# Attention, expert and relative-attention layers on one core: the first ten groups of heads in written order on all engines, with the expert weights' loads among them and zero products on TensorE ahead

## The chip, the cores and the metric

The kernel runs on one core of one Trainium2 chip. A core has TensorE (PE, matrix products, with a sequencer of weight loads shown as PEld), VectorE (DVE), ScalarE (ACT), GpSimd (POOL) and SyncE (SP, which here issues transfers). The metric is the time of one execution on the device in microseconds (us); a kernel's time is the median of its runs. A second figure, the span, runs from the first to the last instruction of the profiled execution.

## The reference

An input x of 16 batches x 256 tokens x 128 channels goes through four layers, each added back to x and each fed by a layer norm of x. All arithmetic is in float32.

```python
x = x + attn_a(layernorm(x))   # 16 heads of 8 channels, weights alpha * sign(W)
x = x + ffn(layernorm(x))      # 8 experts of 512, gates cut at the k-th value of all logits
x = x + attn_b(layernorm(x))   # 16 heads, relative position embedding
x = x + ffn(layernorm(x))
# attn_a:
Wb = mean(abs(W), axis=1) * (W + (sign(W) - W))
q, k, v = (split_heads(x @ Wb.T + b) for ...)
y = softmax(q @ k.T * 8**-0.5) @ v;  out = y @ Wpb.T + bp
# ffn:
gates = logits * (logits >= kth_value_of_all_logits)
out = sum over e of gates[e] * (gelu(x @ w1[e].T + b1[e]) @ w2[e].T + b2[e])
```

The expert weights w1 and w2 are the same in both ffn layers, 2 MB each.

## The kernel before

The program is one straight stream of instructions per engine, with semaphores between them. It loads x as 16 tiles (x0 to x15, one a batch), and keeps all of x and all weights in SBUF. Constants and small vectors come as one tile, `head`.

Attention a (the function `attention_a`) works in 64 *groups*: group i is batch i // 4 and four of its 16 heads (j = 0 to 3), each in 32 rows of PE's array. For group i the code issues

- `scores`: eight products q by k (tile a_s), and on DVE one maximum per head (a_nm, L356);
- one group later, in `visit`, `maxima`: PE turns the maxima (a_mx) and DVE adds them to q (a_qa, L371);
- two groups later `exponentials`: eight products with the sides exchanged (a_t, L379) and the exponential on ACT (a_pT, L385);
- every second group, `values`: 32 products with a_va, a tile of values spread into the 32-row places of the heads.

Beside that, `visit` puts in each batch's own steps by the table at L492: `project` (q and k of the next batch; ACT writes a_qkc, SP sends it to DRAM and, in four transfers, back into the spread tile a_qk), `project_v` and `channels`, `tokens`, `turn_back`, `project_out`, and the gate's steps. `normalise(b)` makes the layer norm of a batch: statistics and aggregates on DVE (L138, L139), then `ve` and `rstd` on POOL (L142, L143), then `xn` on POOL, or for batch 0 on DVE (L146).

Ahead of group 0 stands a preparation. POOL clears wS_q, wS_k, the maxima's tiles a_nm and three tiles a_va, and fills two spread tiles a_qk (L198, L199). DVE makes the signs of the weights in `weights` (sgn_qk, and for values and output sgn_vp): the sign in two instructions, two of `sign - W + W`, one multiply by alpha per weight. PE turns the result (wT_qk, L253), DVE writes it spread into wS_q and wS_k (L257), ACT writes it plain as wq and wk (L263). Batch 0 is turned (a_lnT, L279), copied as a_xnT, and projected by `project_first` (a_pq and a_pk, L315) directly into its spread tile, four products for q and four for k, with biases bqs_ and a_bk_. At group 2 the value and output weights' turned signs (wT_vp) are made and batch 0's values projected (a_pv, L334).

What sets the order: PE's instructions stand in the order in which the code issues them (`manual_schedule` for PE covers all of attention a). POOL's order is written for its first fills and normalisations only. All other engines' orders are chosen by the framework's scheduler, which moves an instruction forward when it takes its operands to be there. Each engine then executes strictly in its own order. The loads of x go over SP's queue one after the other, then b_w (the second attention's weights, 256 KB), w1 and w2; a_w0, head, a_bp and b_bo go over ACT's queue.

After attention a come the first expert layer (h_unit L983 and y_unit L994, 128x512 products, with a search for the k-th logit on DVE at its start), attention b and the second expert layer. In the search the tile flips is a cast of the constants `digits` (L1047), once in each expert layer.

Of the kernel before, what the change touches and what calls it, by code (L numbers as in the profile page):

```python
# [77 lines left out]
def hybrid_kernel(ctx: ExitStack, tc: tile.TileContext, io):  # L78
# [20 lines left out]
            a_w.append(load("a_w1", [P, 2, C], nc.sync, io["a_w"][:, 2:4]))  # L99
    a_bp = load("a_bp", [P, C], nc.scalar, io["a_bp"].partition_broadcast(P))  # L100
    b_bo = load("b_bo", [P, C], nc.scalar, io["b_bo"].partition_broadcast(P))
    b_w = load("b_w", [P, 4, C], nc.sync)
    w1 = load("w1", [P, NE * HID], nc.sync)
    w2 = load("w2", [P, NE * NHC, C], nc.sync)
    wb = {n: b_w[:, i, :] for i, n in enumerate("qkvo")}

    def const(name):
# [18 lines left out]
    def evac(dst, src, on_act):  # L126
        if on_act:
            nc.scalar.copy(dst, src)
        else:
            nc.vector.tensor_copy(dst, src)  # L130

    def normalise(b, last=None):

        n = T // P
        stats = small.tile([P, n, 6], F32, tag="stats", name=f"stats{b}")
        mv = small.tile([P, n, 2], F32, tag="mv", name=f"mv{b}")
        for t in range(n):
            nc.vector.bn_stats(stats[:, t, :], xs[b][:, t, :])  # L138
            nc.vector.bn_aggr(mv[:, t, :], stats[:, t, :])  # L139
        ve = small.tile([P, n], F32, tag="ve", name=f"ve{b}")  # L140
        rstd = small.tile([P, n], F32, tag="rstd", name=f"rstd{b}")
        nc.gpsimd.tensor_scalar(ve, mv[:, :, 1], EPS, None, ALU.add)  # L142
        nc.gpsimd.tensor_tensor(rstd, ve, power, ALU.pow)  # L143
        xn = small.tile([P, n, C], F32, tag="xn", name=f"xn{b}")
        for t in range(n):
            (last or nc.gpsimd).tensor_scalar(  # L146
                xn[:, t, :], xs[b][:, t, :], mv[:, t, 0:1], rstd[:, t : t + 1],
                ALU.subtract, ALU.mult,
            )
        return xn  # L150
# [28 lines left out]
    def attention_a(place, filling):  # L179
# [4 lines left out]
        with ExitStack() as st:  # L184
# [34 lines left out]
                    "p m (j e) -> p m j e", e=32  # L219
                )  # L220

            wS, nms = {}, []
            with tc.manual_schedule(engines={mybir.EngineType.Pool}):
# [9 lines left out]
                with tc.high_priority():  # L233
                    xns = {0: normalise(0, nc.vector)}
                xns[1] = normalise(1)

            def weights(names, w, spread_too):

                alpha = small.tile([P, 2], F32, tag="alpha", name=f"alpha_{names}")
                nc.vector.tensor_reduce(  # L240
                    alpha, w, AX.X, ALU.add, apply_absolute_value=True
                )
                nc.vector.tensor_scalar(alpha, alpha, 1.0 / C, None, ALU.mult)
                s = pool.tile([P, 2, C], F32, tag="sg", name=f"sgn_{names}")
                nc.vector.tensor_scalar(s, w, 0.0, 1.0, ALU.is_gt, ALU.subtract)
                nc.vector.scalar_tensor_tensor(s, w, 0.0, s, ALU.is_ge, ALU.add)

                nc.vector.tensor_tensor(s, s, w, ALU.subtract)
                nc.vector.tensor_tensor(s, s, w, ALU.add)
                pt = psum.tile([P, 2, T], F32, tag="x", name=f"wT_{names}", bufs=8)[:, :, 0:C]  # L250
                for i, n in enumerate(names):
                    nc.vector.tensor_scalar(s[:, i], s[:, i], alpha[:, i : i + 1], None, ALU.mult)
                    nc.tensor.transpose(pt[:, i, :], s[:, i, :], ident)  # L253
                for i, n in enumerate(names):
                    scale = SCALE if n == "q" else 1.0
                    if spread_too:
                        nc.vector.tensor_scalar(  # L257
                            wS[n][:, :, :, 1 : 1 + DH],
                            pt[:, i].rearrange("p (g j d) -> p g j d", g=NG, j=NJ),
                            scale, None, ALU.mult,  # L260
                        )
                    wT[n] = wpool.tile([P, C], F32, tag=f"w{n}", name=f"w{n}")
                    nc.scalar.activation(wT[n], pt[:, i], AF.Copy, scale=scale)  # L263

            bq = wpool.tile([P, 1], F32, tag="bqs", name="bqs")
            nc.vector.tensor_scalar(bq, a_bq, SCALE, None, ALU.mult)
            bq_ = wpool.tile([P, NG], F32, tag="bqs_", name="bqs_")
            nc.vector.tensor_scalar(bq_, a_bq_, SCALE, None, ALU.mult)

            q, k, va, xnT, qaug, probs, heads, ys, yTs = ({} for _ in range(9))  # L270

# [5 lines left out]
            def channels(b, pt):  # L277
                for t in range(2):
                    nc.tensor.transpose(pt[:, t * P : (t + 1) * P], xns[b][:, t, :], ident)  # L279
                yield  # L280
                xnT[b] = pool.tile([P, T], F32, tag="xnT", name=f"a_xnT{b}")
                evac(xnT[b], pt, b > 0)

            def project(b):

# [20 lines left out]
            def project_first():  # L306

                to = spread[0]
                q[0], k[0] = to[:, 0], to[:, 1]
                for half in range(2):  # L310
                    for i, (n, bias) in enumerate((("q", bq_), ("k", a_bk_))):
                        pp = psum.tile([P, 2, T], F32, tag="x", name=f"a_p{n}_{half}", bufs=8)
                        for j in range(2):
                            g = 2 * half + j
                            nc.tensor.matmul(  # L315
                                pp[:, j, :], wS[n][:, g].rearrange("p j e -> p (j e)"),
                                xnT[0], start=True, stop=True,
                            )
                        for j in range(2):
                            g = 2 * half + j  # L320
                            if i:
                                nc.vector.tensor_scalar(
                                    to[:, i, g], pp[:, j, :], bias[:, g : g + 1], None, ALU.add
                                )
                            else:
                                nc.scalar.activation(
                                    to[:, i, g], pp[:, j, :], AF.Identity,
                                    bias=bias[:, g : g + 1], scale=1.0,
                                )

            def project_v(b, pv):
                pv = pv.rearrange("p (t c) -> p t c", c=C)
# [149 lines left out]
            spread_tile(False)  # L482
            together(channels(0, half_bank("a_lnT0")))
            weights("qk", a_w[0], True)
            project_first()
            for i in range(2):
                spread_tile(True)
                values_tile()
# [35 lines left out]
            for i in range(NG * (NB + 2) + 1):  # L524
                b, s = divmod(i, NG)
                for half in range(2):
                    parts = []
                    if i < n:
                        parts += [scores(i, 2 * half + j) for j in range(2)]
                    if 2 <= i < n + 2:  # L530
                        parts += [exponentials(i - 2, 2 - 2 * half + j) for j in range(2)]
                    together(*parts)
                    if not i and not half:
                        together(channels(1, half_bank("a_lnT1")))
                if i >= n + 2:
                    place["h"] = (epool, 5, psum, "x", 8)
                    place["y"] = (psum, "x", 8)
                    place["raw"] = (epool, 4)
                    for _ in range(own_at.get(i - n, 0)):
                        own.append(next(filling))  # L540
                if i == 2:
                    weights("vp", a_w[1], False)
                    pv = psum.tile([P, 2, T], F32, tag="x", name="a_pv0", bufs=8)
                    together(project_v(0, pv[:, 0]))
                visit(i)
                if i == 0:
                    xns[2] = normalise(2)
                if s == 3 and of(b + 3):
                    xns[b + 3] = normalise(b + 3)

# [469 lines left out]
    def experts(last, place, raw, filling, middle):  # L1020
        with ExitStack() as st:
# [19 lines left out]
            def search():  # L1041
# [1 line left out]


                digits = const("digits")
                flips = small.tile([P, len(SHIFTS) * NCAND], I32, tag="flips", name="flips", bufs=1)
                nc.vector.tensor_copy(flips, digits)  # L1047

                pc = count((0.0, 2.0, -2.0 + 2.0**-23), "s")
                ok = small.tile([P, 3], F32, tag="ok_s", name="ok_s")  # L1050
# [234 lines left out]
```

## Time and profile before

| | |
|---|---|
| three timed runs | 1556.63, 1557.60, 1558.27 us; median 1557.6 |
| profiled execution | 1556.52 us |
| its span | 1554.7 us |
| PE busy | 1522.4 us (98%) |
| DVE busy | 814.6 us (52%) |
| ACT busy | 833.0 us (54%) |
| POOL busy | 404.3 us (26%) |
| granted clock of PE, mean | 0.999 |
| read from and written to DRAM | 50.88 MB, 12.58 MB |

A line of the page or of an answer names the engine, the line of the kernel, the operation, and output<-inputs by the program's names without buffer numbers. In a timeline a line starts with the start and the duration of a merged run of instructions, in us, and ends with the idle time before it and what ended it. In a table of stages each engine has its busy time and in brackets its number of instructions; PEclk is the clock that PE was granted, 1.00 being full; then follow the mean busy share of the 16 DMA engines and what they moved in GB/s. A matmul in float32 stands in the trace as two records, so "x4" are two products.

### The profile page before, as it was taken

What the parts mean: (1) busy time and instruction counts of PE and PEld (TensorE: products, weight loads), DVE (VectorE), ACT (ScalarE), POOL (GpSimd) and SP (SyncE); (2) the same over time, 40 slices, a digit from 0 to 9 for tenths busy, and PEclk for the clock granted to TensorE, in tenths of its full rate; (3) what the DMA queues carried; (4) which work ended last, traced back from release to release, by engine and by line L of the source; (5) the groups of instructions that cost most, each with busy time, mean ns of one, the idle gap of its engine ahead of it and who ended that gap; (6) DMA issues with size and microseconds to landing.
All of it is one profiled execution on the core that took longest, in us unless ns stands there. A gap on an engine that the chain in (4) does not pass through costs nothing. (4 is left out here: it accounts for less than half of the span.)

```text
span 1554.7 us, 30891 instructions
## 1 busy us (share of the span) xinstructions
PE 1522.4 (98%) x12274; PEld 857.3 (55%) x12274; DVE 814.6 (52%) x1646; ACT 833.0 (54%) x2073; POOL 404.3 (26%) x518
## 2 busy tenths in 40 slices
PE   5999999999999999999999999999999999999998
PEld 3777777644444444444577777777544444444444
DVE  5788878635224322221599999999364133222122
ACT  2666666544443343434588888888644434343342
POOL 6123322100001000003188888897100000000000
PEclk9999999999999999999999999999999999999999
DMA  6111111000322211111122222222002233221110
GB/s 197 29 36 35 29 29 36 9 8 0 71 58 72 68 37 38 40 35 41 22 53 47 47 53 56 54 52 44 8 1 39 54 78 88 56 44 40 46 40 7
DMA packets 174127, 69.91 MB, mean 45 GB/s; under 512 B 74520, under 2 KB 173600, under 8 KB 173728
## 3 DMA queue, kind: packets, MB, share of 16 engines
q1 hardware_dynamic: 173408, 67.54, 18.7%
q8 instruction: 97, 1.59, 0.4%
q10 hardware_dynamic: 576, 0.41, 0.1%
q14 instruction: 46, 0.38, 0.1%
HBM read 50.88 MB, written 12.58 MB: 41 GB/s over the span
## 5 line engine op out<-in xcount | busy, mean ns | idle before, releaser
L985 ACT ACTIVATE hT<-ph,head 128x512 f32<-128x512 f32 x512 | 351.3, 687 | 420.8 <-PE ph L983 418.3
L983 PE MATMUL ph<-xn,w 128*128 128x512 f32 x1024 | 464.5, 594 | 1.1 <-ACT hT L985 1.1
L994 PE MATMUL py<-hT,w 128*128 128x512 f32 (+1 forms) x1040 | 461.3, 586 | 1.0 <-ACT logits L884 0.5
L994 PEld LDWEIGHTS py<-hT,w 128*128 128x128 f32 x1040 | 196.6, 190 | 237.3 <-issue 230.5
L983 PEld LDWEIGHTS ph<-xn,w 128*128 128x128 f32 x1024 | 191.3, 190 | 228.0 <-issue 224.2
L1110 DVE SCALAR_TENSOR_TENSOR gy<-py,head,gb 128x512 f32<-128x512 f32 x82 | 61.6, 751 | 425.4 <-PE py L994 419.2
L798 ACT ACTIVATE b_pr<-b_s,b_nm 128x256 f32<-128x256 f32 x512 | 235.9, 474 | 58.8 <-DVE b_nm L793 58.6
L356 DVE TENSOR_REDUCE a_nm<-a_s 128x2 f32<-128x512 f32 x256 | 160.4, 686 | 55.3 <-PE a_t L379 37.3
L793 DVE TENSOR_REDUCE b_nm<-b_s 128x4 f32<-128x1024 f32 x128 | 152.7, 1193 | 16.5 <-PE b_s L783 16.4
L783 PE MATMUL b_s<-b_kT,b_qd 64*64 64x256 f32 x1024 | 159.9, 382 | 0.4 <-ACT b_pr L798 0.2
L385 ACT ACTIVATE a_pT<-a_t 128x512 f32<-128x512 f32 x256 | 133.2, 599 | 48.2 <-PE a_t L379 47.5
L808 DVE STREAM_TRANSPOSE b_pT<-b_pr 128x1024 f32<-128x1024 f32 x128 | 157.2, 1228 | 0.0
L783 PE MATMUL b_s<-strip,b_qb 64*64 64x256 f32 x2048 | 156.6, 376 | 0.0
L783 PE MATMUL b_s<-b_kS,b_qd 64*64 64x256 f32 x1024 | 156.5, 382 | 0.0
L351 PE MATMUL a_s<-a_qk 32*128 32x256 f32 x1024 | 135.1, 391 | 0.0
L673 POOL TENSOR_TENSOR b_qd<-b_qsel,head 128x512 f32<-128x512 f32 x64 | 84.2, 1337 | 179.4 <-DMA b_qsel<-b_qT 170.7
L142 POOL TENSOR_SCALAR ve<-mv 128x2 f32<-128x2 f32 x64 | 15.0, 234 | 442.6 <-DVE mv L139 441.9
L379 PE MATMUL a_t<-a_qa,a_qk 32*128 32x256 f32 x1024 | 122.9, 397 | 3.5 <-DVE a_qa L371 2.7
L798 ACT ACTIVATION_READ_ACCUMULATOR b_pr<-b_s,b_nm 128x1 f32 x512 | 104.3, 204 | 0.0
L351 PEld LDWEIGHTS a_s<-a_qk 32*128 32x128 f32 x1024 | 91.7, 186 | 22.5 <-issue 15.2
L146 POOL TENSOR_SCALAR xn<-x,mv,rstd 128x128 f32<-128x128 f32 x126 | 99.8, 801 | 6.1
L783 PEld LDWEIGHTS b_s<-strip,b_qb 64*64 64x64 f32 x2048 | 78.3, 133 | 32.2
(175 smaller groups left out, 1438.9 us busy)
## 6 DMA issues: line engine op xcount, KB each, us to landing
gb<-gd SPq DMA_DIRECT2D x128, 256.0 KB
w<-in_w SPq DMA_DIRECT2D x2, 2048.0 KB
a_qks<-a_qkc SPq DMA_DIRECT2D x15, 256.0 KB
a_qk<-a_qks SPq DMA_DIRECT2D x60, 64.0 KB
x<-in_x SPq DMA_DIRECT2D x16, 128.0 KB
b_qs<-b_qT SPq DMA_DIRECT2D x64, 32.0 KB
b_qsel<-b_qT SPq DMA_DIRECT2D x64, 32.0 KB
b_z<-b_qs SPq DMA_DIRECT2D x16, 128.0 KB
```

What stands on the lines that cost most here:

```text
L146: (last or nc.gpsimd).tensor_scalar(xn[:, t, :], xs[b][:, t, :], mv[:, t, 0:1], rstd[:, t : t + 1], ALU.subtract, ALU.mult,)
L351: nc.tensor.matmul(sc[:, t, :], q[b][rows, g, t * P : (t + 1) * P], k[b][rows, g, :], start=True, stop=True,)
L356: nc.vector.tensor_reduce(nms[G % 4][:, :, j, 0:1].rearrange("p t o -> p (t o)"), sc, AX.X, ALU.max, negate=True,)
L379: nc.tensor.matmul(sc[:, t, :], k[b][rows, g, t * P : (t + 1) * P], qaug[G][rows, :], start=True, stop=True,)
L385: nc.scalar.activation(pT, sc, AF.Exp)
L783: nc.tensor.matmul(sc[64 * c : 64 * c + 64, r, u, :], (qb_[rows, at, c] if rel else qd[rows, at, x]).rearrange("p h q -> p (h q)"), strip[ ...
L793: nc.vector.tensor_reduce(nm, sc, AX.X, ALU.max, negate=True)
L798: nc.scalar.activation(pr[:, u, r, :], sc[:, r, u, :], AF.Exp, bias=nm[:, r, u : u + 1], scale=1.0, accum_out=sums[b][:, n : n + 1],)
L808: nc.vector.transpose(pT[:, half % 2, 4 * i : 4 * i + 4].rearrange("p n k h q -> p (n k h q)"), probs.pop(U).rearrange("p u r k -> p (u r ...
L983: nc.tensor.matmul(ph, w1[:, m * P : (m + 1) * P], xn2[c], start=True, stop=True)
L985: nc.scalar.activation(hT, ph, AF.Gelu_apprx_tanh, bias=b1[:, m : m + 1], scale=1.0)
L994: nc.tensor.matmul(py[:, 0:width], w2[:, e * NHC + k, :], hs[k], start=k == 0, stop=k == NHC - 1)
```

## The change

The preparation becomes one function, `begin`, and from there until group 10 DVE, ACT, POOL and SP too execute in the order in which the code issues their instructions; `written.close()` ends that at group 10. The written order is: the fills on POOL up to the first a_va; five products on PE of the cleared tile wS_q by itself into a tile that nobody reads; statistics of batch 0 and the start of the signs of q and k on DVE; batch 0's `xn`, on DVE, in another form of instruction; its turning on PE and copy, now on ACT; the rest of the signs, with one multiply by alpha for both weights instead of one each; biases; batch 1's normalisation; wS_q and wS_k; the projections, with the two parts of the value and output weights' signs between them. Their multiply by alpha and their turning come at group 2. Spread tiles 1 and 2 and a_va 1 and 2 are filled after batch 1's normalisation.

Batch 2 is normalised after group 1 instead of after group 0. b_w and w1 are loaded at group 5, w2 at group 9, where flips is now also cast, once for both expert layers. In every normalisation the statistics of both halves now come ahead of both aggregates.

```diff
-    b_w = load("b_w", [P, 4, C], nc.sync)
-    w1 = load("w1", [P, NE * HID], nc.sync)
-    w2 = load("w2", [P, NE * NHC, C], nc.sync)
+    b_w = cpool.tile([P, 4, C], F32, tag="b_w", name="b_w")
+    w1 = cpool.tile([P, NE * HID], F32, tag="w1", name="w1")
+    w2 = cpool.tile([P, NE * NHC, C], F32, tag="w2", name="w2")
+    flips = cpool.tile([P, len(SHIFTS) * NCAND], I32, tag="flips", name="flips")
+    def load_later(step):
+        for name, t in ((("b_w", b_w), ("w1", w1)), (("w2", w2),))[step]:
+            nc.sync.dma_start(t, io[name])
+        if step:
+            nc.vector.tensor_copy(flips, const("digits"))
...
+    def statistics(b):
...
         for t in range(n):
             nc.vector.bn_stats(stats[:, t, :], xs[b][:, t, :])
+        for t in range(n):
             nc.vector.bn_aggr(mv[:, t, :], stats[:, t, :])
...
-            def weights(names, w, spread_too):
+            def weights(names, w):
...
                 nc.vector.scalar_tensor_tensor(s, w, 0.0, s, ALU.is_ge, ALU.add)
+                yield
                 nc.vector.tensor_tensor(s, s, w, ALU.subtract)
                 nc.vector.tensor_tensor(s, s, w, ALU.add)
+                yield
+                nc.vector.tensor_tensor(
+                    s, s, alpha.unsqueeze(2).to_broadcast([P, 2, C]), ALU.mult
+                )
                 pt = psum.tile([P, 2, T], F32, tag="x", name=f"wT_{names}", bufs=8)[:, :, 0:C]
+                for i in range(2):
+                    nc.tensor.transpose(pt[:, i, :], s[:, i, :], ident)
+                yield pt
...
+            def begin():
+                fills()
+                warm = psum.tile([P, 2, T], F32, tag="x", name="a_warm", bufs=8)
+                for _ in range(5):
+                    nc.tensor.matmul(
+                        warm[:, 0], wS["q"][:, 0].rearrange("p j e -> p (j e)"),
+                        wS["q"][:, 0:2].rearrange("p g j e -> p (g j e)"),
+                        start=True, stop=True,
+                    )
+                mv, rstd = statistics(0)
+                qk = weights("qk", a_w[0])
+                next(qk)
+                xns[0] = small.tile([P, T // P, C], F32, tag="xn", name="xn0")
+                for t in range(T // P):
+                    nc.vector.scalar_tensor_tensor(
+                        xns[0][:, t, :], xs[0][:, t, :], mv[:, t, 0:1],
+                        rstd[:, t : t + 1].to_broadcast([P, C]), ALU.subtract, ALU.mult,
+                    )
+                together(channels(0, half_bank("a_lnT0")))
+                next(qk)
+                pt = next(qk)
+                nc.vector.tensor_scalar(bq, a_bq, SCALE, None, ALU.mult)
+                nc.vector.tensor_scalar(bq_, a_bq_, SCALE, None, ALU.mult)
+                xns[1] = normalise(1)
...
+                keep("qk", pt)
+                vp = weights("vp", a_w[1])
+                spread_tile(False)
...
+                        if i:
+                            next(vp)
...
+                return vp
...
-                evac(xnT[b], pt, b > 0)
+                nc.scalar.copy(xnT[b], pt)
...
-            weights("qk", a_w[0], True)
-            project_first()
+            written = st.enter_context(ExitStack())
+            written.enter_context(
+                tc.manual_schedule(
+                    engines={
+                        getattr(mybir.EngineType, e) for e in ("DVE", "Activation", "Pool", "SP")
+                    }
+                )
+            )
+            vp = begin()
...
-                    weights("vp", a_w[1], False)
+                    keep("vp", next(vp))
...
-                if i == 0:
+                if i == 1:
                     xns[2] = normalise(2)
+                if i in (5, 9):
+                    load_later(i // 9)
+                if i == 10:
+                    written.close()
...
-                flips = small.tile([P, len(SHIFTS) * NCAND], I32, tag="flips", name="flips", bufs=1)
-                nc.vector.tensor_copy(flips, digits)
```

Left out of `begin` are the two instructions on DVE that write wS_q and wS_k, and the loop of the former `project_first`, in which the two `next(vp)` stand between the products for k and the copies out of them.

More of the change, by code (lines that the diff above doesn't have):

```diff
@@ L130, in evac @@
             nc.vector.tensor_copy(dst, src)
-    def normalise(b, last=None):
+    def statistics(b):
         n = T // P
@@ L143, in normalise @@
         nc.gpsimd.tensor_tensor(rstd, ve, power, ALU.pow)
-        xn = small.tile([P, n, C], F32, tag="xn", name=f"xn{b}")
-        for t in range(n):
+        return mv, rstd
+    def normalise(b, last=None):
+        mv, rstd = statistics(b)
+        xn = small.tile([P, T // P, C], F32, tag="xn", name=f"xn{b}")
+        for t in range(T // P):
             (last or nc.gpsimd).tensor_scalar(
@@ L220, in of_heads, with fills @@
                 )
-            wS, nms = {}, []
-            with tc.manual_schedule(engines={mybir.EngineType.Pool}):
+            wS, nms, xns = {}, [], {}
+            bq = wpool.tile([P, 1], F32, tag="bqs", name="bqs")
+            bq_ = wpool.tile([P, NG], F32, tag="bqs_", name="bqs_")
+            def fills():
                 for n in "qk":
@@ L232, in attention_a @@
                 values_tile()
-                with tc.high_priority():
-                    xns = {0: normalise(0, nc.vector)}
-                xns[1] = normalise(1)
-            def weights(names, w, spread_too):
+            def weights(names, w):
                 alpha = small.tile([P, 2], F32, tag="alpha", name=f"alpha_{names}")
@@ L251, in weights, with keep @@
+                yield pt
+            def keep(names, pt):
                 for i, n in enumerate(names):
[L252 to L261, printed above, removed]
-                    wT[n] = wpool.tile([P, C], F32, tag=f"w{n}", name=f"w{n}")
-                    nc.scalar.activation(wT[n], pt[:, i], AF.Copy, scale=scale)
@@ L265, in attention_a @@
[L265 to L268, printed above, removed]
+                    wT[n] = wpool.tile([P, C], F32, tag=f"w{n}", name=f"w{n}")
+                    nc.scalar.activation(
+                        wT[n], pt[:, i], AF.Copy, scale=SCALE if n == "q" else 1.0
+                    )
@@ new lines, in begin @@
+            def begin():
[11 more added lines that the diff above has]
+                xns[0] = small.tile([P, T // P, C], F32, tag="xn", name="xn0")
+                for t in range(T // P):
+                    nc.vector.scalar_tensor_tensor(
[8 more added lines that the diff above has]
+                xns[1] = normalise(1)
+                for i, n in enumerate("qk"):
+                    nc.vector.tensor_scalar(
+                        wS[n][:, :, :, 1 : 1 + DH],
+                        pt[:, i].rearrange("p (g j d) -> p g j d", g=NG, j=NJ),
+                        SCALE if n == "q" else 1.0, None, ALU.mult,
+                    )
+                keep("qk", pt)
+                vp = weights("vp", a_w[1])
+                spread_tile(False)
+                to = spread[0]
+                q[0], k[0] = to[:, 0], to[:, 1]
+                for half in range(2):
+                    for i, (n, bias) in enumerate((("q", bq_), ("k", a_bk_))):
+                        pp = psum.tile([P, 2, T], F32, tag="x", name=f"a_p{n}_{half}", bufs=8)
+                        for j in range(2):
+                            g = 2 * half + j
+                            nc.tensor.matmul(
+                                pp[:, j, :], wS[n][:, g].rearrange("p j e -> p (j e)"),
+                                xnT[0], start=True, stop=True,
+                            )
+                        if i:
+                            next(vp)
+                        for j in range(2):
+                            g = 2 * half + j
+                            if i:
+                                nc.vector.tensor_scalar(
+                                    to[:, i, g], pp[:, j, :], bias[:, g : g + 1], None, ALU.add
+                                )
+                            else:
+                                nc.scalar.activation(
+                                    to[:, i, g], pp[:, j, :], AF.Identity,
+                                    bias=bias[:, g : g + 1], scale=1.0,
+                                )
+                return vp
@@ L304, in project @@
                 q[b], k[b] = to[:, 0], to[:, 1]
[L306 to L329, printed above, removed]
             def project_v(b, pv):
@@ L481, in attention_a @@
             n, own = NB * NG, []
-            spread_tile(False)
-            together(channels(0, half_bank("a_lnT0")))
-            weights("qk", a_w[0], True)
-            project_first()
+            written = st.enter_context(ExitStack())
[4 more added lines that the diff above has]
+                    }
+                )
+            )
+            vp = begin()
             for i in range(2):
```

## The prediction

> **What bounds the kernel now.** I read the page's busy shares first, then the stages, then the first 36 us engine by engine.
>
> ```profile
> PE 1522.4 (98%) x12274; PEld 857.3 (55%) x12274; DVE 814.6 (52%) x1646; ACT 833.0 (54%) x2073; POOL 404.3 (26%) x518
> ```
>
> TensorE (PE) is busy for all but 32.3 us of 1554.7. So a change can win idle time, or time in which PE is slow; the stages tell where either is (columns: us; busy PE, weight loads, DVE, ACT, POOL with counts; clock, DMA share, GB/s).
>
> ```profile
> 0.00:15.54 15.54, 0.00 (x0) 0.00 (x0) 9.19 (x39) 1.28 (x1) 13.54 (x30) 1.00 0.81 209
> 15.54:22.00 6.46, 5.98 (x22) 4.52 (x22) 2.34 (x8) 2.11 (x6) 6.17 (x10) 1.00 1.01 426
> 22.00:30.00 8.00, 6.04 (x49) 3.85 (x52) 6.27 (x11) 1.23 (x4) 4.21 (x6) 0.98 0.45 180
> 30.00:36.00 6.00, 4.97 (x41) 4.05 (x37) 2.85 (x5) 2.90 (x7) 0.00 (x0) 0.74 0.25 34
> 40.00:50.00 10.00, 9.87 (x138) 6.73 (x132) 5.88 (x11) 5.75 (x12) 0.00 (x0) 1.00 0.18 46
> ```
>
> From group 3, at 36.2 us, PE is full and stays so. All that can be won in one place lies before. PE's waits there:
>
> ```profile
> PE a_lnT L279 <- DVE xn L146: 15.5, 1, 15.5
> PE a_t L379 <- DVE a_qa L371: 2.0, 1, 2.0
> PE a_pv L334 <- ACT wv L263: 1.0, 1, 1.0
> PE a_pq L315 <- DVE wS_q L257: 0.5, 1, 0.5
> ```
>
> PE's first work waits until DVE has normalised batch 0. DVE's timeline tells why that is late:
>
> ```profile
> 3.65 0.49 DVE L138 BATCH_NORM_STATS2 stats<-x 128x6 f32<-128x128 f32 x2 [3.65 <-DMA x<-in_x]
> 8.87 0.29 DVE L138 BATCH_NORM_STATS2 stats<-x 128x6 f32<-128x128 f32 x1 [2.64 <-DMA x<-in_x]
> 11.13 2.07 DVE L252 TENSOR_SCALAR sgn_qk<-sgn_qk,alpha_qk 128x128 f32<-128x128 f32 x2
> 14.47 0.47 DVE L252 TENSOR_SCALAR sgn_vp<-sgn_vp,alpha_vp 128x128 f32<-128x128 f32 x2
> 15.14 0.60 DVE L146 TENSOR_SCALAR xn<-x,mv,rstd 128x128 f32<-128x128 f32 x2
> ```
>
> The statistics come at 3.65, and POOL ends rstd at 6.61 (5.89 + 0.72). Between lie a wait for a later batch (2.64), scaling of signs beside POOL's copy and memset (2.07, where its twin takes 0.47), and value weights and statistics that nobody needs yet. So about 8.5 us is order alone. PE's timeline, last:
>
> ```profile
> 17.18 2.04 PE L315 MATMUL a_pq<-a_xnT,wS_q 128*128 128x256 f32 x4 [0.48 <-DVE wS_q L257]
> 20.11 1.03 PE L315 MATMUL a_pq<-a_xnT,wS_q 128*128 128x256 f32 x4
> 21.93 1.13 PE L351 MATMUL a_s<-a_qk 32*128 32x256 f32 x8
> 26.95 0.70 PE L351 MATMUL a_s<-a_qk 32*128 32x256 f32 x4
> 29.61 0.73 PE L379 MATMUL a_t<-a_qa,a_qk 32*128 32x256 f32 x2 [1.96 <-DVE a_qa L371]
> 36.21 0.48 PE L351 MATMUL a_s<-a_qk 32*128 32x256 f32 x2
> ```
>
> The same projection takes 2.04 at first and 1.03 three microseconds later, so PE starts at half rate, though the clock column reads 1.00 there. After the 1.96 us wait it falls to half again:
>
> ```profile
> 29.00:30.00 1.00, 0.39 (x4) 0.42 (x8) 0.47 (x2) 0.00 (x0) 0.00 (x0) 0.86 0.24 72
> 30.00:31.00 1.00, 1.00 (x14) 0.98 (x13) 0.17 (x1) 0.00 (x0) 0.00 (x0) 0.50 0.57 90
> 33.00:34.00 1.00, 0.66 (x4) 0.20 (x2) 0.70 (x2) 0.62 (x2) 0.00 (x0) 0.93 0.09 16
> ```
>
> 0.28 + 3 + 0.14 = 3.42 us at 0.50.
>
> **The change part by part**, as times at which PE reaches four marks: first projection (17.18 before), first scores (21.93), first exponentials' product a_t (29.61), group 3 (36.21).
>
> *First projection.* Statistics start at 3.65 as before; both aggregates end at 4.4. POOL: ve 0.23, rstd 0.72 and three hand-overs of 0.1 end at 5.6. Beside it DVE does the sign start of q and k: reduce 0.39, scale 0.15, 0.30, 0.41, to 5.65. The normalisation in its new form isn't in the trace: taken at its old 0.60 per pair (bounds 0.5 and 0.8, twice the 256-wide form at 0.41), to 6.25. PE turns it in 0.44 (row at full rate) to 0.73 (at half rate); ACT, idle for 13.15 us there, copies it in 0.37: ready by 7.4, hidden. DVE goes on: 0.41, 0.48 and one 256-wide multiply (0.41 as its neighbours) to 7.55; PE turns the weights (0.44 to 0.63) to 8.1. DVE meanwhile has two small biases (0.12 each; the second was 0.83 beside POOL's copy, which now comes later) and batch 1's statistics (0.46 + 0.3), to 8.55; wS_q 0.29, hand-over 0.15: 9.0. Gain 8.2, or 7.5 with the bias at 0.83.
>
> *The zeros.* Five 128x256 products. The row at 17.18 makes one 0.92 at half rate (1.83 for two, up to the next start at 19.01), so 4.6 us after wS_q is cleared (0.75 + 0.53 = 1.28): 1.4 to 6.0, before the first transpose at 6.3. No delay. Do they raise the clock for the projections? Between 6.0 and 9.0 PE has two short bursts, 0.9 to 1.4 us of work in 3. Before, 1.5 us of work in the 3.4 ahead of 29.72 was followed by half rate. So I expect the clock to be won and mostly lost again: projections take 4.75 as before (17.18 to 21.93, 2.3 of it at half rate). Bounds: 8 x 0.43 = 3.5 at full rate (the row at 20.11), 8 x 0.92 = 7.3 at half rate. Scores at 13.75.
>
> [...]
>
> *Scores to a_t.* DVE's order is kept: four reductions, four more, then a_qa. So 7.68 stays, and with it the wait of 1.96. The two-input sign steps now run beside POOL's fills: up to 1.1 more (the 2.07 row less 0.47, per instruction 0.8, rounded up), of which DVE's 0.83 of idle ahead of the second four takes most. Nothing taken, 0.8 kept in the range. a_t at 21.45.
>
> *a_t to group 3.* Before 6.60, at half rate, with the value weights' signs long done. Now their last multiply stands on DVE behind group 2's reductions, and PE's transposes, wv and project_v wait for it, with the maxima of group 1 queued behind on PE. At half rate the reductions end 5.0 after a_t (33.30 + 1.29 less 29.61), the multiply at 5.4, transposes at 5.9, wv at 6.3, and 1.52 from project_v to group 3 (34.69 to 36.21): 7.9. At full rate the reductions end at 3.7: 6.5. The same gap as before speaks for half rate, its position in a 3.4 us window is open: 7.4 taken. Group 3 at 28.83 instead of 36.21: **7.4 gained**.
>
> *What I cost at nothing.* Batch 2's statistics on DVE move in front of group 2's reductions, batches 3 and 4 behind groups 3 and 7: 0.56 + 0.34 = 0.9 each, in DVE's idle of 1.23 and 1.56 before the reductions of groups 3 and 4; without that cover up to 2.7. POOL's fills (7.5 us from 11.2) end at 18.7; batch 1's spread needs the first at 20.5, and batch 2's normalisation (2.8) ends near 25, needed at 28. ACT's order changes by one copy. On SP b_w and w1 go behind batch 2's five transfers, w2 behind batch 3's; the first matmul on w1 is at 306.4, so they have 240 us. SP waits for none of them. flips: a cast of 0.18 instead of two. Statistics before aggregates, everywhere: off the path.
>
> The profiled execution took 1556.52, 1.82 beyond its span and 1.1 below the median of 1557.6. Its own time less 7.4 is 1549.1; from the median it would be 1550.2; I say **1549.6**.
>
> **Rivals.**
> - *The clock holds* from the zeros on, and through the wait: 3.5 and 6.5, group 3 at 26.7, 9.5 gained, 1547.0. For it: 4.6 us of unbroken work. Against: the row at 30 us.
> - *Zeros that raise no clock*, projections wholly at half rate, and DVE's collision with the fills: 7.3, 8.5 and 7.9, group 3 at 32.7, 3.5 gained, 1553.0. For it: nothing in the trace shows PE on zeros. Against: before, 2.3 us of real work sufficed.
> - *DVE loses its cover* in groups 3 to 10: 2.7 back, and with the low clock of the rival above the kernel is within 0.2% of before, 1555.7. Against: 0.3 to 0.6 of idle is left at each place.
> - *The weights starve PE.* They now arrive while PE is full, near 36 and 53 us, and PE's instructions come over the same engines ("q8 instruction: 97, 1.59, 0.4%" in the page). If PE stood through 4.35 MB at 430 GB/s, 10.1 us, and began at half rate after each (2 x 1.7), the loss of 13.5 makes 1562.6, slower; it decides from 10.5 of the 13.5. Against: in 18 to 22 us PE was full with the same loads at 377 to 475 GB/s.
> - *The order is not the cause of the late start*: PE would wait for x0's or the weights' arrival. Against: statistics ran at 3.65, the weights' reduction at 4.14.
>
> **How the numbers follow.** Forecast 0.52; clock holds 0.18; half rate throughout 0.14; cover lost 0.08; starved 0.06; arrival as the cause 0.02. 0.2% of 1557.6 is 3.1 us, about what a measurement of this kernel tells from no change. Faster: the first three, 0.84; within 0.2%: lost cover and arrival, 0.10; slower: 0.06. The range leaves out the last three: from 1546.5 (clock holds, and 0.5 for hand-overs and a multiply that I may have made too long) to 1553.0 (half rate). The forecast's own is 1548 to 1551.5.
>
> **What would show it.** PE's first rows are five products at about 1.4; its first transpose near 6.3, first projection near 9.0, a_s near 13.8, a_t near 21.5 with a wait of about 2 before it, group 3 near 28.8; a wait of PE for the value weights of about 2 instead of 1.0. From there each group as long as before. It is wrong if PE's idle time in 36 to 70 us grows, or if the first projection is later than 10.

## The result and the profile after

The changed kernel takes 1552.34 us (median of six runs, 1551.5 to 1552.98) against 1558.15 for the kernel before (1556.63 to 1558.89). The ratio is 0.9963 with a 95% interval of 0.9950 to 0.9975: 5.8 us or 0.37% faster, clear of the 0.2% that a measurement can tell. The forecast was 1549.6, between 1546.5 and 1553.0; the time lies in that range, but outside the 1548 to 1551.5 that the prediction calls the forecast's own.

The busy shares of the changed kernel, from its page, and its stages (us; busy PE, weight loads, DVE, ACT, POOL; clock, DMA share, GB/s):

```profile
PE 1530.6 (99%) x12284; PEld 862.1 (56%) x12284; DVE 809.3 (52%) x1642; ACT 833.3 (54%) x2074; POOL 403.7 (26%) x518
```

```profile
0.00:6.00 6.00, 4.63 (x10) 3.20 (x10) 2.04 (x9) 1.28 (x1) 4.42 (x15) 1.00 0.57 138
6.00:12.00 6.00, 4.59 (x12) 3.22 (x13) 3.94 (x17) 1.66 (x5) 3.35 (x5) 1.00 0.91 241
12.00:20.00 8.00, 8.00 (x50) 5.48 (x48) 5.26 (x11) 2.05 (x5) 6.08 (x10) 1.00 0.17 45
20.00:28.00 8.00, 3.91 (x41) 2.80 (x40) 6.11 (x14) 2.51 (x6) 3.37 (x5) 0.99 0.30 68
28.00:34.00 6.00, 5.86 (x63) 4.34 (x65) 2.79 (x5) 3.10 (x7) 0.00 (x0) 0.73 0.00 0
```

In what follows, the rate is the clock granted to PE, which the traces show at half (0.50, from 27.86 to 31.28 in the changed kernel) and at full (1.00).

PE's busy time grew by 8.2 us while the kernel became shorter: 4.6 us of it are the zeros, and products at half rate count longer (a pair of projections 1.91 to 2.04, against 1.03 in the kernel before at full rate). PE's idle time now lies between 20 and 28 us, where it is busy for 3.91 of 8, and the stage behind it has a mean clock of 0.73. PE's waits behind the first projection, up to 100 us, longest first:

```profile
PE a_t L429 <- DVE a_qa L421: 2.0, 1, 2.0
PE wT_vp L272 <- DVE sgn_vp L267: 1.8, 1, 1.8
PE a_pv L384 <- ACT wv L279: 0.4, 1, 0.4
```

PE's first transpose, which waits for batch 0's normalisation, starts at 6.16 instead of 15.54, and the zeros fill most of the time before it; a new wait of 1.8 stands at the value weights. DVE's timeline shows both:

```profile
3.73 0.49 DVE L147 BATCH_NORM_STATS2 stats<-x 128x6 f32<-128x128 f32 x2 [3.73 <-DMA x<-in_x]
5.75 0.61 DVE L300 SCALAR_TENSOR_TENSOR xn<-x,mv,rstd 128x128 f32<-128x128 f32 x2 [0.15 <-POOL rstd L153]
23.54 2.53 DVE L406 TENSOR_REDUCE a_nm<-a_s 128x2 f32<-128x512 f32 x4 [0.29 <-PE a_s L401]
25.99 0.41 DVE L267 TENSOR_TENSOR sgn_vp<-sgn_vp,alpha_vp 128x256 f32<-128x256 f32 x1
```

And PE's timeline at the marks of the prediction:

```profile
1.33 4.63 PE L290 MATMUL a_warm<-wS_q 128*128 128x256 f32 x10 [1.33 <-POOL wS_q L245]
6.16 0.73 PE L354 MATMUL a_lnT<-head,xn 128*128 128x128 f32 x2 [0.19 <-DVE xn L300]
8.84 2.04 PE L326 MATMUL a_pq<-a_xnT,wS_q 128*128 128x256 f32 x4 [0.48 <-DVE wS_q L311]
12.38 1.91 PE L326 MATMUL a_pq<-a_xnT,wS_q 128*128 128x256 f32 x4
14.09 1.09 PE L326 MATMUL a_pk<-a_xnT,wS_k 128*128 128x256 f32 x4
15.11 1.13 PE L401 MATMUL a_s<-a_qk 32*128 32x256 f32 x8
22.79 0.48 PE L429 MATMUL a_t<-a_qa,a_qk 32*128 32x256 f32 x2 [1.96 <-DVE a_qa L421]
26.55 0.41 PE L272 MATMUL wT_vp<-head,sgn_vp 128*128 128x128 f32 x2 [1.77 <-DVE sgn_vp L267]
29.71 0.80 PE L401 MATMUL a_s<-a_qk 32*128 32x256 f32 x2
34.84 0.48 PE L401 MATMUL a_s<-a_qk 32*128 32x256 f32 x2
```

All five products of zeros ran at half rate (0.93 each), and so did six of the eight projections: the third pair takes 1.91, and only the last, at 14.09, takes 1.09. Group 4 begins at 34.84; in the kernel before it began at 40.59:

```profile
40.59 0.48 PE L351 MATMUL a_s<-a_qk 32*128 32x256 f32 x2
```

So the front gained 5.75 us in this pair of profiles. The medians differ by as much, but that is in part chance, since each profile is one execution and the rate changes at other places in others, as the experiments show.

The two profiled spans differ by less, 3.9 (1554.7 and 1550.8). Matched product by product, the lead is 5.7 at 120 us and still 5.7 at the first product of attention b (754.67, before 760.34); from 759 on it is 4.0. There, at the passage from the first expert layer to attention b, the profiled run of the changed kernel had a stretch at half rate that the profiled run of before had not (first the kernel after, then the kernel before):

```profile
755.00:760.00 5.00, 5.00 (x52) 2.89 (x54) 0.54 (x1) 2.22 (x3) 0.24 (x1) 0.67 0.14 16
```

```profile
760.00:765.00 5.00, 4.67 (x72) 3.28 (x76) 1.50 (x2) 2.48 (x4) 0.90 (x1) 1.00 0.15 17
```

PE's order of work there is the same in both kernels; two profiles of one kernel, among the experiments below, differ in the same way. The profiled execution of before, at 1556.52, was quicker than any of its timed runs.

### The profile page after: what moved, and what is told of

The parts are those of the page before. It is cut to its first block, busy times and chain, and to the rows that moved or that the text cites. A ratio compares the mean times of both kernels' runs of the same rounds, so it can differ in the third digit from the quotient of the medians.

```text
span 1550.8 us, 30900 instructions
## 1 busy us (share of the span) xinstructions
PE 1530.6 (99%) x12284; PEld 862.1 (56%) x12284; DVE 809.3 (52%) x1642; ACT 833.3 (54%) x2074; POOL 403.7 (26%) x518
```

## The experiments

Theory: the gain is DVE's order at the start, which puts batch 0's normalisation at 5.75 instead of 15.14; the zeros bring nothing; the late multiply of sgn_vp takes some of it back. Rivals: the zeros, the rewritten steps or the later loads carry it.

**The zeros taken out**

```diff
-                warm = psum.tile([P, 2, T], F32, tag="x", name="a_warm", bufs=8)
-                for _ in range(5):
-                    nc.tensor.matmul(
...
```

> The changed kernel without the five products of zeros. Theory (the gain is the engines' order; the zeros bring nothing): in the changed kernel's trace the zeros run at half rate from 1.33 to 5.96 and the projections stay at half rate until 14.1, so the full rate is owed to the projections themselves. First transpose at 6.2, first projection at 8.8 as with the zeros; the rate rises somewhere between 11.9 and 15.3, first scores between 13.9 and 15.7; time within 0.7 us of the changed kernel, ratio to before 0.996 to 0.997. Rival (the zeros count as work and bring the rise of the rate forward): the rise comes a window of 3.4 us later, first scores 1.8 us later (near 16.9), time 1.8 us longer.

1552.12 us, ratio 0.9964 (0.9951 to 0.9977): no difference in time from the changed kernel. First transpose at 6.14, first projection at 8.82, scores at 14.41, within the range given. The rate rose at 12.8. In this profile it then fell from 23.1 to 33.3, and group 4 came at 36.16, 1.3 later than in the changed kernel's; the medians do not show that. So the five zeros bring nothing that the time shows. That zeros do not count as work for the clock does not follow, as the next two experiments show.

**The zeros alone, in the kernel before**

```diff
+            warm = psum.tile([P, 2, T], F32, tag="x", name="a_warm", bufs=8)
+            for _ in range(5):
+                nc.tensor.matmul(
+                    warm[:, 0], wS["q"][:, 0].rearrange("p j e -> p (j e)"),
+                    wS["q"][:, 0:2].rearrange("p g j e -> p (g j e)"),
+                    start=True, stop=True,
+                )
             spread_tile(False)
```

> The kernel before with the five products of zeros alone. Theory and rival agree: they end near 6, PE's first real work comes at 15.5, far more than a window of 3.4 us later; first projection at 17.2, scores between 21 and 24, time as before within 0.1%. It excludes that the zeros by themselves make any of the 5.8 us.

1557.36, ratio 1.0004 (0.9995 to 1.0012): no change, as both expected. But its stages show the clock at work (same columns as above):

```profile
8.00:9.00 1.00, 0.00 (x0) 0.00 (x0) 0.27 (x2) 0.00 (x0) 1.00 (x2) 1.00 1.02 292
9.00:10.00 1.00, 0.00 (x0) 0.00 (x0) 1.00 (x5) 0.00 (x0) 1.00 (x2) 0.63 0.97 266
19.00:20.00 1.00, 1.00 (x5) 0.86 (x4) 0.00 (x0) 0.81 (x3) 1.00 (x2) 0.75 1.04 442
```

In the kernel before the column read 1.00 here, since the trace has no record of the clock before its first change, at 19.48. In this run the trace's clock records have a rise at 5.85, a fall at 9.26, 3.30 us after the zeros ended at 5.96, and a rise at 19.50. So the clock rose at 5.85 with products of zeros as PE's only work; here nothing used it before it was lost.

**Zeros without a break up to the projections**

```diff
+                zero = nms[3].rearrange("p t j e -> p (t j e)")
+                def idle(n, width=T):
+                    for _ in range(n):
+                        nc.tensor.matmul(
+                            warm[:, 0, 0:width], zero[:, 0:P], zero[:, 0:width],
+                            start=True, stop=True,
+                        )
+                idle(5)
...
                 together(channels(0, half_bank("a_lnT0")))
+                idle(1)
                 next(qk)
                 pt = next(qk)
+                idle(1, P)
```

The five products on wS_q are replaced by `idle(5)`; POOL clears the maxima's tiles ahead of wS_q and wS_k (not printed here). Two short breaks remained: 0.40 us ahead of the first transpose and 0.35 ahead of the first projection.

> The changed kernel with two more products of zeros, one (256 columns) behind batch 0's transposes and one (128 columns) behind the weights' transposes, so that PE has no idle time from 1.4 until the projections; the zeros come from a cleared maxima tile. If products of zeros count as work for the clock, the rate rises at the latest two windows after 1.4, by 8.2, the eight projections run in 3.5 instead of 6.3, first scores come near 12.4 instead of 15.1, and the time falls by 2.7 to about 1549.6. If they do not count, the rate rises as before between 11.9 and 15.3 and the time stays at 1552.3 within 0.7, at worst 0.1 longer for the added products.

PE's timeline of this kernel:

```profile
6.67 0.91 PE L294 MATMUL a_warm<-a_nm 128*128 128x256 f32 x2
8.68 1.10 PE L333 MATMUL a_pq<-a_xnT,wS_q 128*128 128x256 f32 x4 [0.35 <-POOL ve L152]
11.34 1.03 PE L333 MATMUL a_pk<-a_xnT,wS_k 128*128 128x256 f32 x4
12.30 1.13 PE L408 MATMUL a_s<-a_qk 32*128 32x256 f32 x8
24.57 0.66 PE L273 MATMUL wT_vp<-head,sgn_vp 128*128 128x128 f32 x2 [1.74 <-DVE sgn_vp L268]
```

The rate rose at 7.3, all projections ran at full rate (1.03 to 1.10 a pair, 1.91 to 2.04 for the first three of the changed kernel), scores came at 12.30 (12.4 expected). The zeros count. "At the latest two windows after 1.4" was the author's estimate, twice the 3.42 us at half rate of the kernel before; no run shows such a limit. The time is 1549.54, as expected, ratio 0.9952 (0.9941 to 0.9964); that interval overlaps the changed kernel's, so the gain of 2.8 is shown at the mark and only likely in the time (2.8 by the medians, 1.7 by the ratios). In the profiled run much of it went again:

```profile
21.00:22.00 1.00, 1.00 (x16) 0.97 (x10) 1.00 (x2) 0.89 (x2) 0.90 (x2) 0.50 0.56 53
31.00:32.00 1.00, 1.00 (x14) 0.53 (x10) 1.00 (x3) 0.82 (x3) 0.00 (x0) 0.90 0.00 0
```

From 21.0 to 31.2, three times 3.41 us, the clock was at half, across the waits for a_qa and the value weights. Group 4 came at 34.05, only 0.8 ahead of the changed kernel.

**The rewritten steps in the scheduler's order**

```diff
-            written.enter_context(
-                tc.manual_schedule(
-                    engines={
-                        getattr(mybir.EngineType, e) for e in ("DVE", "Activation", "Pool", "SP")
-                    }
-                )
-            )
```

> The changed kernel without the written order on DVE, ACT, POOL and SP: all its rewritten steps and the zeros stay, the scheduler chooses the order. Batch 0's normalisation then stands behind the statistics of batches 2 to 4 and the value weights' signs on DVE again. Theory (order is the cause): first transpose of batch 0 near 15, group 4 near 40 (40.6 before, 34.8 in the changed kernel), time 1557 to 1558.5. Rival (the rewritten steps, or the later loads of the expert weights, carry the gain): first transpose well before 12 and half or more of the 5.8 us kept, time under 1555.3.

1555.95, ratio 0.9986 (0.9976 to 0.9996): 1.8 of the 5.8 remain, so neither theory nor rival in full. DVE's, POOL's and then PE's timeline:

```profile
7.69 0.96 DVE L260 TENSOR_SCALAR sgn_vp<-a_w 128x256 f32<-128x256 f32 x1
9.05 0.29 DVE L147 BATCH_NORM_STATS2 stats<-x 128x6 f32<-128x128 f32 x1 [0.33 <-DMA x<-in_x]
11.92 0.61 DVE L300 SCALAR_TENSOR_TENSOR xn<-x,mv,rstd 128x128 f32<-128x128 f32 x2
```

```profile
8.47 1.41 POOL L153 TENSOR_TENSOR rstd<-ve,power 128x2 f32<-128x2 f32 x2
```

```profile
12.32 0.74 PE L354 MATMUL a_lnT<-head,xn 128*128 128x128 f32 x2 [6.70 <-DVE xn L300]
```

The normalisation is again behind the value weights and the statistics of batches 2 to 4, and batch 0 arrived half a microsecond late (at 4.25), but it comes at 11.92 instead of 15.14: the scheduler met the later batches with a wait of 0.33 instead of 2.64, and one instruction beside POOL's copy lost 0.66 (0.96, against 0.30 in the changed kernel) where two lost 1.6. DVE's order is not all of it: POOL, too, in the scheduler's order, does other work first and ends its first rstd only at 9.22, where that ended at 5.71 in the changed kernel. Group 4 came at 39.46. So the written order makes some two thirds of the gain by the medians; the rest comes with the rewriting, by way of another order that the scheduler finds for it. How much that rest is, the interval leaves open: 0.6 to 3.7 us.

**The value weights early**

```diff
                 nc.vector.tensor_tensor(s, s, w, ALU.add)
-                yield
                 nc.vector.tensor_tensor(
                     s, s, alpha.unsqueeze(2).to_broadcast([P, 2, C]), ALU.mult
                 )
+                yield
...
                 if i == 2:
-                    keep("vp", next(vp))
...
                 if i == 1:
                     xns[2] = normalise(2)
+                    keep("vp", next(vp))
```

> The changed kernel with the multiply of sgn_vp moved on DVE directly behind its additions (in DVE's idle near 14.3), and the turning of the value weights and their copies wv and wp moved into the end of group 1, where PE waits 2 us for a_qa anyway. Theory (the late multiply costs the 1.8 and 0.4 us of PE's waits, and through them the second fall to half rate, which stood at 27.9 to 31.3 in the changed kernel and 23.1 to 33.3 in the one without zeros): group 3 starts at 26 to 27 instead of 29.7, group 4 near 31 instead of 34.8; 2.2 us from the waits and up to 1.7 from the rate, time 1549 within 0.8. Rival (DVE's reductions are the bound there, so that PE waits for a_qa of group 1 as long as it now waits for the weights): group 3 at 29 or later, time 1552.

1544.98, ratio 0.9927 (0.9914 to 0.9939): 4 us better than the 1549 expected. PE's timeline:

```profile
12.25 1.13 PE L401 MATMUL a_s<-a_qk 32*128 32x256 f32 x8
17.17 0.38 PE L272 MATMUL wT_vp<-head,sgn_vp 128*128 128x128 f32 x2
19.83 0.48 PE L429 MATMUL a_t<-a_qa,a_qk 32*128 32x256 f32 x2 [1.65 <-DVE a_qa L421]
24.92 0.48 PE L401 MATMUL a_s<-a_qk 32*128 32x256 f32 x2
29.29 0.48 PE L401 MATMUL a_s<-a_qk 32*128 32x256 f32 x2
```

The wait for the weights is gone; the longest left is the 1.65 for a_qa. In this run the same five zeros raised the clock at 6.7, so scores came at 12.25; that part is not the edit's. A cleaner comparison is the repeat below, whose rate rose at 14.4, much as in the changed kernel's profile (14.2). Its marks:

```profile
15.21 1.13 PE L401 MATMUL a_s<-a_qk 32*128 32x256 f32 x8
26.47 0.48 PE L401 MATMUL a_s<-a_qk 32*128 32x256 f32 x2
30.84 0.48 PE L401 MATMUL a_s<-a_qk 32*128 32x256 f32 x2
```

From the scores (15.21, there 15.11) it is 11.26 to group 3 (there 14.60) and 15.63 to group 4 (there 19.73). So the late multiply cost 3.3 us up to group 3 and 4.1 up to group 4 in this pair. Its two waits are 2.1 of that; the stretch at half rate behind them, 3.41 us, accounts for up to 1.7 more.

In the repeat the rate did not fall in these groups. In the first run it fell once, from 20.3 to 23.8; there it is 17.04 from the scores to group 4, and the cost comes to 2.7. The time says more than either mark: by the ratios of the two runs, 0.9927 and 0.9923 against 0.9963, it is some 6 us. Fewer slow stretches fit that (granted clocks of 0.998 to 0.999 in these runs, 0.995 to 0.998 in the changed kernel's), but the difference was not tested apart.

**Both, and both with group 0's maxima ahead**

```diff
+                if i == 1:
+                    held = [scores(1, j) for j in range(NJ)]
+                    for pair in (held[:2], held[2:]):
+                        for _ in range(2):
+                            for g in pair:
+                                next(g)
+                    pt = psum.tile([P, 2, T], F32, tag="x", name="a_mx0", bufs=8)
+                    together(maxima(0, pt[:, 0]))
+                    together(*held)
...
```

The kernel with both joins the edits of the zeros without a break and of the value weights early. What takes these scores and maxima out of their former place is not printed here.

> Products of zeros without a break up to the projections, and the value weights early. If the two gains add (2.8 for the projections at full rate, 3 to 4 for the value weights and the second fall): scores at 12.3, exponentials' product a_t at 20.0, group 3 near 23.8, group 4 near 28.2, time 1545.5 within 1. If the clock only moves its slow stretch to another place, group 4 comes after 31 and the time stays above 1548.

> As the kernel with both, and group 0's maxima are turned and added to q ahead of group 1's four reductions on DVE instead of behind them. Theory (the 2 us wait ahead of a_t is DVE's order again): a_t starts near 17.9 instead of 20.0 and the wait of 2 us goes; but DVE then has twelve reductions in a row, and group 3 gains only 0.5 to 1 (near 23.0), time 0.5 to 1 below the kernel with both, near 1545; with the wait gone the fall of the clock goes too. Rival (the wait only moves to PSUM banks or to a_qa of group 1): group 3 and the time as with both.

Both: 1545.64, ratio 0.9923 (0.9911 to 0.9936). Scores at 12.23, a_t at 19.82, group 3 at 24.89 (23.8 expected), group 4 at 29.26 (28.2 expected); the clock still fell once, from 21.2 to 24.6. In time it is not to be told from the value weights early alone.

With the maxima ahead: 1544.31, ratio 0.9922 (0.9909 to 0.9934), the lowest median of all. DVE's timeline:

```profile
14.25 2.47 DVE L413 TENSOR_REDUCE a_nm<-a_s 128x2 f32<-128x512 f32 x4
17.51 0.42 DVE L428 TENSOR_TENSOR a_qa<-a_qk,a_mx 128x256 f32<-128x256 f32 x1 [0.80 <-PE a_mx L422]
17.85 2.48 DVE L413 TENSOR_REDUCE a_nm<-a_s 128x2 f32<-128x512 f32 x4
```

a_t starts at 17.99 and the wait for a_qa is gone; the clock did not fall once in this profile after its rise at 6.1. Group 3 gains 0.8 (24.05), as expected, and the time 1.3 in the medians, inside the intervals.

**The expert weights loaded early again**

```diff
+    for name, t in (("b_w", b_w), ("w1", w1), ("w2", w2)):
+        nc.sync.dma_start(t, io[name])
...
-        for name, t in ((("b_w", b_w), ("w1", w1)), (("w2", w2),))[step]:
-            nc.sync.dma_start(t, io[name])
```

> The changed kernel with b_w, w1 and w2 loaded at the start behind x, as in the kernel before. Theory (the loads are hidden either way): first projection at 8.8, batch 1's spread tiles arrive in time since the loads end near 25 and group 4 starts at 34.8; time as the changed kernel within 0.7 us. Rival (the later loads save PE or the transfers of batch 1 something): the transfers of a_qks and a_qk, issued near 19.6 and 21.8, land behind the weights, after 26, and group 4 waits; time more than 1 us longer.

1552.15, ratio 0.9968 (0.9957 to 0.9979): the loads' place costs and brings nothing that the time shows. SP's timeline, of this kernel and of the changed one:

```profile
16.81 0.38 SPq L371 DMA_DIRECT2D a_qks<-a_qkc  x1
26.78 1.35 SPq L375 DMA_DIRECT2D a_qk<-a_qks  x4
```

```profile
19.64 0.37 SPq L371 DMA_DIRECT2D a_qks<-a_qkc  x1
21.82 1.36 SPq L375 DMA_DIRECT2D a_qk<-a_qks  x4
```

The rival's first half is true: batch 1's q and k wait 10.0 us behind the weights instead of 2.2. Its second half is not: group 4, which needs them, starts at 33.70 and waits for nothing. With the value weights early it would start at 29.3, when the four transfers issued at 26.78 might not have landed; that was not tried.

In this profile, too, the zeros raised the clock early (6.4), scores came at 12.28, and the clock fell twice, 20.0 to 23.5 and 26.9 to 30.3. Of the lead of 2.8 at the scores, 1.1 was left at group 4.

**With the value weights early: without zeros, and a repeat**

```diff
-                warm = psum.tile([P, 2, T], F32, tag="x", name="a_warm", bufs=8)
-                for _ in range(5):
...
```

> The changed kernel with the value weights early and without any product of zeros. [...] Theory A (the zeros bring something only where nothing loses the rate again): without them scores come at 13.9 to 15.7 and the time is 1.5 to 2.8 longer than with them, 1546.5 to 1547.8, still 4 us below the changed kernel. Theory B (the zeros bring nothing at all in the median, since the rate falls again over the wait for a_qa in any case): time 1545 as with them, within 0.7.

> The same with the five zeros again, on the same chip, as its companion: 1545 within 0.7.

Without zeros 1547.27, ratio 0.9932 (0.9919 to 0.9944); with them 1546.16, 0.9923 (0.9909 to 0.9936), on the same chip, where 1545 within 0.7 was expected. In the two profiles the zeros did nothing for the rate: it rose at 11.7 without them and at 14.4 with them, and the scores came at 13.89 and 15.21. The 1.1 us in favour of the zeros lie inside the intervals: between theory A (1.5 to 2.8) and theory B (under 0.7), and not settled.

## Why the prediction was right, and where its terms were off

**First projection.** 9.0 said, 8.84 measured: the order on DVE, the hand-overs and the new form of the normalisation (0.61 for 0.60) came as worked out. That is the mechanism of the whole, and it held: 8.34 us were won up to this mark.

**The zeros.** No delay, as said: they ended at 5.96, before the transpose at 6.16. "I expect the clock to be won and mostly lost again" was wrong: in the profiled run it was not won at all. In the two profiles of kernels with the same start in which it was won before the projections (value weights early, early loads), it was kept, and the scores came 3.6 us after the first projection. So 4.75 lies between two outcomes, 3.6 and 6.3, and is neither. The term "projections take 4.75 as before" is the mis-sized one: 6.27 (8.84 to 15.11), inside its bounds of 3.5 and 7.3. The scores were 1.36 late: 1.52 more here, less the 0.16 that the first projection was early.

The clock's own records, from which the column of the clock is averaged, show what went before its changes. Between two changes they last 13.653, 3.413, 723.626, 3.413 and 791.892 us in the changed kernel and 10.240, 3.413 and 1522.344 in the kernel before. In a stretch as long as the shortest of them ahead of the rise, 3.41 us, PE was busy for 2.94 in the kernel before (up to 19.48), for 3.41 here (up to 14.21) and throughout with the zeros alone (up to 5.85). The same length up to 7.38 and up to 10.80 here holds 2.73 and 2.65 of work, and the rate did not rise there. "2.3 us of real work sufficed" had counted the projections alone: the 2.94 ahead of 19.48 hold the weights' transposes too. Of the six profiles of kernels with just these zeros, four show the early rise (5.1 in the scheduler's order, 5.9 with the zeros alone, 6.4 with the early loads, 6.7 with the value weights early) and two don't; what decides between them no run shows.

**Scores to a_t.** 7.68 said and measured, with the wait of 1.96 unchanged, and DVE's reductions not hindered by POOL's fills (2.72, as before).

**a_t to group 3.** 7.4 said, 6.92 measured. The new wait for the value weights is the one described (1.77 + 0.37, "about 2 instead of 1.0"). But the clock fell behind this wait, at 27.86, not behind the one for a_qa, and so the slow stretch came later and lay across group 3 (one-microsecond stages of the changed kernel):

```profile
27.00:28.00 1.00, 0.68 (x5) 0.68 (x6) 0.00 (x0) 0.44 (x2) 0.00 (x0) 0.93 0.07 16
28.00:29.00 1.00, 1.00 (x7) 1.00 (x6) 0.40 (x1) 0.39 (x1) 0.00 (x0) 0.50 0.00 0
31.00:32.00 1.00, 1.00 (x20) 0.86 (x20) 0.37 (x1) 0.29 (x1) 0.00 (x0) 0.86 0.00 0
```

The 3.41 us before the fall at 27.86 hold 1.28 us of work; those before the fall at 29.72 in the kernel before held 1.45, those before the fall at 754.90 here 1.72. Those from 21.04 to 24.45 here, with the wait for a_qa, hold 1.67, and the clock stayed. So the falls came after little work, which goes with the prediction's reason for the fall, too little work in 3.4 us, but these stretches show no limit. "Its position in a 3.4 us window", on which the 7.4 leans, is shown by no run: the 7.4 was the author's choice between 6.5 and 7.9, and the runs showed the fall 5.07 us after a_t (22.79 to 27.86), where it came 0.11 after it before (29.61 to 29.72), and 6.92 up to group 3. Group 3, begun at 29.71 in the slow stretch, took 0.75 longer (5.13 to group 4, where 4.38 was its length before). "From there each group as long as before" was wrong for this one group, and with it the front's gain is 5.75, not 7.4: 1.36 too little at the scores, 0.48 better than said up to group 3, 0.75 lost in it.

**How much of it was luck.** The cause and the way were right, and the size was within the range because that reached to 1553.0, the rival with half rate throughout; the measured 1552.34 is nearer to that rival than to 1549.6. The forecast also leant on a quick execution of the kernel before: 7.4 below its median of six runs would be 1550.75. Of the smaller slips, 4.46 MB of weights instead of 4.35, 7.8 instead of 7.9 for the sum at half rate and 21.43 instead of 21.45 for a_t, none changes the outcome.

**What was costed at nothing.** Loads: shown by the early loads. Statistics and fills: the wait for a_qa is the same 1.96, and groups 4 to 10 keep their length (group 5 at 38.41 is 5.75 ahead of 44.16, group 10 at 60.25 is 5.76 ahead of 66.01). "The clock holds" did not come about here; the rate held from its early rise only in the kernel with both and the maxima ahead. "DVE loses its cover" is refuted: the groups keep their length. "The order is not the cause" is refuted by the early start itself, 15.54 to 6.16, and by the scheduler's order, which puts it back to 12.32. "Zeros that raise no clock" is refuted by the zeros alone (rise at 5.85) and the unbroken zeros (7.3), though the profiled run looked like it. "The weights starve PE" is refuted: PE was busy for 9.87 of each 10 us from 40 to 70, with the loads at 43 and 62, and for 9.73 to 9.87 before.

## What to carry to other kernels

When an engine's start waits for one product of a long chain, look for how much foreign work its in-order queue puts in front: here 8.5 us, of which the change won nearly all up to the first projection, while its own order put a new late step (a multiply behind four reductions) in front of PE, worth 2.7 to 4.1 us at group 4. A wait on the matrix engine of two microseconds can cost more than its length, since here the rate could fall behind it (a wait of 1.77, then half rate from 27.86 to 31.28), 1.7 us lost in each such 3.41 us; so of two placements for a small step choose the one in a wait that is there anyway. Warming products of 4.6 us raised the rate in four of six profiles; with the breaks behind them filled they did so in all three. In the time, the five zeros alone brought nothing that the runs show, and filling the breaks a gain that is only likely: further on the rate fell again (from 21.0 to 31.2 with the unbroken zeros, from 21.2 to 24.6 with both).

## What the runs showed of the hardware that was not expected

The clock rose with products of zeros: with them alone at 5.85, and with the breaks filled at 7.3, while in the profiled run of the changed kernel, with the same five, it rose only at 14.21. Of the 2.94 us of work ahead of the rise at 19.48 in the kernel before, 0.63 are transposes; whether they count as the projections do was not tried.

Whether the passage at 755 us loses the clock differs between runs of one kernel: of the two profiles with the value weights early, the second fell there (751.6 to 755.1) and the first did not. The changed kernel's profile shows it too (754.90 to 758.32), that of the kernel before does not. It cost 1.7 us of the changed kernel's lead, so two profiles should be compared mark by mark before their spans are.

Mean granted clocks in the timed runs were 0.995 to 0.998 for the changed kernel, 0.996 to 1.000 for the one before and 0.999 to 1.000 for the one with value weights and maxima ahead. A stretch of 3.41 us at half rate is 1.7 us of 1550, or 0.0011: some two to four such stretches in a run of the changed kernel, none or one in the last. These means are not to be compared across kernels without care: what lies ahead of the first change of the clock counts as 1.00, so the half rate up to 19.48 in the kernel before does not show in them. With the zeros alone added, which bring the first change to 5.85 in the profile, the means are 0.992 to 0.998 at the same time.
